# Softmax sums of an attention kernel: a chain of accumulating transfers, one meeting on TensorE, and the division on VectorE in PSUM

## The chip, the cores and the metric

The kernel runs on one core of a Trainium2 chip. The metric is device time in microseconds (us) of one execution; the time before is the median of three runs. A separate execution was recorded by the hardware profiler; all durations of single instructions come from that one. The engines are called PE (TensorE, matrix products), DVE (VectorE), ACT (ScalarE), POOL (GpSimd) and SP (the queue that issues most of the loads). Each engine works through its own instructions in the order in which the program wrote them, and waits on semaphores for the others.

## The reference

Two sequences of 2048 tokens with 512 features pass through a pre-norm attention layer and a small feed-forward layer.

```python
q = rope(layernorm(x) @ wq + bq)          # 16 heads of 32
k, v = rope(... @ wk + bk), ... @ wv + bv # 2 groups, each used by 8 heads
scores = einsum('bqhd,bkhd->bhqk', q * hd**-0.5, k) * hd**-0.5
attn = softmax(scores, axis=-1)
x = x + einsum('bhqk,bkhd->bqhd', attn, v) @ wo + bo
x = x + fp8_matmul(layernorm(x), weight)  # both operands rounded to e4m3
```

The softmax divides by the sum of the exponentials over all 2048 keys. The change is about how this sum is formed and how the division is done.

## The kernel before

**Tiling.** The tokens are cut into 8 blocks of 512 queries, and the 16 heads into 4 quads of 4 heads. A *unit* is one half block (256 queries) of one quad, so there are 64 units (`units`, L470). A unit runs over its 2048 keys in 4 *rounds* (`r` = 0 to 3, L994) of 4 chunks of 128 keys each. The main loop is L978 to L1034 and is unrolled; before it comes the projection of keys and of the first queries, and after it the last norms and the feed-forward layer.

**One chunk.** PE computes the scores of 4 heads into the PSUM tile `T` (L963), ACT writes `p = exp(T)` into SBUF, 128 keys x 4 heads x 256 queries (L972), and PE multiplies `p` by the values: `columns` (L905, L913) issues for each chunk 4 products, one for each head, that fill the 4 partition groups of `avs[:, 0, :]`. The four chunks' `columns` stand together at the end of the round (L1024).

**The maximum.** The exponentials need each row's maximum first. A generator, `scores_for_maxima` (L507), computes the scores once more for the *next* unit: PE writes `s` (L517), DVE reduces each to `part` (L524). The main loop advances it by four steps a round, two products and two reductions in each; the fourth step of a round (L1019) stands just before the filled-in jobs and `columns`. The steps run four ahead of the units, so a unit's last reduction, and `mx` (L531), fall in round 2 of the unit before it.

**The sums before.** POOL adds the exponentials of chunks 0 and 1 to `pair`, and of chunks 2 and 3 to a tile of `far_sums` (`add_pair`, L946). A transfer issued from POOL's queue then adds `pair` onto the far sum (L1015, `accum_op=add`), so that each round leaves one far sum. In round 2 one more such transfer adds `far_sums[0]` onto `far_sums[1]` (L1017). Three tiles remain. PE sums them over the 128 keys by products with a matrix of ones (`sum_up`, L923, L927): two of them at the end of the next unit's round 0, the third at the end of its round 1, into `avs[:, 1, :]`. Each tile takes 4 products, and a float32 product is two matmuls in the trace, so a unit has 24 of them.

**The division before.** `finish_heads` (L881) is a generator. When it is made, in round 1, ACT copies the sums from PSUM to SBUF (L885). Its further steps are run by `fill(ON_DVE, 3)` in the next round, round 2: two reciprocals of 128 columns each on DVE in SBUF (L889), and in the second of these steps the product on POOL (L890) that writes `attn_of`. At the end of each unit ACT copies `avs[:, 0, :]` to `both[:, 0, :]` (L1033).

**What sets the order.** The loop is written inside `manual_schedule`: each engine's order is the program's order. `fill` (L763) hands out other work between the fixed parts, one step at a time: first from `finishing`, then from `queue` (projections, output products `po`), then from `beside`. `fill(ON_DVE, ...)` at L1021 runs *after* the fourth scores step and *before* the round's `columns`. Waits between engines are not written by hand; the framework places them from what each instruction reads and writes.

**Buffers.** `avs` is a PSUM tile of 2 x 256 float32 per partition, 2048 bytes, with one buffer: its first half collects the products with the values of unit `u`, its second half the sums of unit `u - 1`. The tiles of `far_sums` have 4 buffers (tag `pa`), `p` has 4.

Of the kernel before, what the change touches and what calls it, by code (L numbers as in the profile page):

```python
# [8 lines left out]
F32 = mybir.dt.float32  # L9
# [4 lines left out]
ALU = mybir.AluOpType  # L14
AX = mybir.AxisListType

P = 128
# [10 lines left out]
def preln_attn_fp8_ffn_kernel(  # L28
# [37 lines left out]
    nc = tc.nc  # L66
# [9 lines left out]
    HB = 256  # L76
# [6 lines left out]
    ON_PE, ON_DVE, OTHER = "PE", "DVE", "other"  # L83
# [9 lines left out]
    w2 = ctx.enter_context(tc.tile_pool(name="w2", bufs=6))  # L93
# [376 lines left out]
    units = [(k, half) for k in range(len(quads)) for half in range(HALVES)]  # L470
# [133 lines left out]
    def finish_block(n, attn):  # L604
        yield OTHER
        xt = x_res.pop(n)
        for i in range(NT):
            yield from add_output(n, xt, attn, i)
        if n < len(y_far):
            nc.sync.dma_start(y_far[n], xt)  # L610
        else:
            y_near[n] = xt
        beside.append(Job(ending(second_norm(n, xt), f"res_{n}")))
        if n == NBLK - 2:
            fetch_y(0, xpool, "x")
            fetch_y(1, wide, "xnT")
            fetch_y(3, wide, "attn", bufs=2)


    def finish_most(n, xt, attn):  # L620
        yield OTHER
        for i in range(NT):
            yield from add_output(n, xt, attn, i, range(DC - 1))

    def finish_rest(n, xt, attn, half):
        yield OTHER
        tiles = range(half * HT, (half + 1) * HT)
        for i in tiles:
            yield from add_output(n, xt, attn, i, range(DC - 1, DC))
        beside.append(Job(second_norm(n, xt, tiles)))  # L630
        y_near[n] = xt
# [128 lines left out]
    finishing = []  # L760
    attn_of = {}

    def fill(kind, pieces=1):  # L763

        for _ in range(pieces):
            ready = [job for job in queue if job.due <= step[0] and not job.waits()]
            if lent[0] is not None:
                ready = [job for job in ready if job is owner[0]]
            able = [
                (jobs, job)  # L770
                for jobs, some in ((finishing, finishing[:1]), (queue, ready), (beside, beside))
                for job in some
                if job.kind in (kind, OTHER) and job.due <= step[0]
            ]
            if able:
                do(*able[0])

    def do(jobs, job):
        held = lent[0]
        job.step()  # L780
        if held is None and lent[0] is not None:
            owner[0] = job
        if job.kind is None:
            jobs.remove(job)
# [93 lines left out]
            fetch_y_over_keys(4, "kS", 0)  # L878
            fetch_y_over_keys(5, "dkS", 0)

    def finish_heads(u, both, sums):  # L881

        k, half = units[u]
        n, quad = quads[k]
        nc.scalar.copy(both[:, 1, :], sums)  # L885
        for c in range(HB // P):
            yield ON_DVE
            piece = both[:, 1, c * P : (c + 1) * P]
            nc.vector.reciprocal(piece, piece)  # L889
        nc.gpsimd.tensor_tensor(  # L890
            attn_of[n][:, quad, half * HB : (half + 1) * HB], both[:, 0, :], both[:, 1, :], ALU.mult
        )
        if n == NBLK - 1:
            if quad == QUADS - 2 and half == HALVES - 1:
                queue.append(Job(finish_most(n, x_res[n], attn_of[n])))
            elif quad == QUADS - 1:
                queue.append(Job(finish_rest(n, x_res[n], attn_of[n], half)))
        elif quad == QUADS - 1 and half == HALVES - 1:
            job = Job(finish_block(n, attn_of.pop(n)))
            if n not in biased:  # L900
                job.due = NEVER
                without_x[n] = job
            queue.append(job)

    def columns(u, chunks, probs, av):  # L905

        k, half = units[u]
        for kc, p in zip(chunks, probs):
            if kc == NTS - 2 and u + 1 < len(units):
                tp = ps_t.tile([P, 4 * HB], F32, tag="E", name=f"mtp_{u + 1}")  # L910
                gather_maxima(u + 1, tp)
            for j in range(4):
                nc.tensor.matmul(  # L913
                    av[j * HD : (j + 1) * HD, :],
                    vX[batch(k)][:, kc, group(k), :],
                    p[:, j, :],
                    start=(kc == 0),
                    stop=(kc == NTS - 1),
                    tile_position=(0, j * HD),
                    skip_group_check=True,  # L920
                )

    def sum_up(dst, parts, start, stop):  # L923

# [12 lines left out]
    def add_pair(u, kc, a, b):  # L937
        far = kc % ROUND == 2
        pa = papool.tile(
            [P, 4, HB],  # L940
            F32,
            tag="pa" if far else "pair",
            name=f"pa_{u}_{kc}",
            bufs=4 if far else 2,
        )
        nc.gpsimd.tensor_tensor(pa, a, b, ALU.add)  # L946
        return pa
# [27 lines left out]
    with tc.manual_schedule():  # L975
        for _ in range(LEAD):
            next(scores)
        for u, (k, half) in enumerate(units):  # L978
            n, quad = quads[k]
            if half == 0 and quad == 0:  # L980
                attn_of[n] = wide.tile(
                    [P, QUADS, TB], F32, tag="attn", name=f"attn_{n}", bufs=2
                )
            stack_next(u)
            banks = [
                ps_t.tile([P, 4, HB], F32, tag="EO"[parity], name=f"T_{u}_{parity}")
                for parity in range(2)
            ]

            far_sums = []  # L990
            whole = u == len(units) - 1
            ending_soon = u >= len(units) - 2
            pieces = 2 if ending_soon else 1
            for r in range(ROUNDS):  # L994
                chunks = list(range(r * ROUND, (r + 1) * ROUND))
                step[0] += 1
                while r == 1 and landing:
                    landing.pop()()
                if r == 2:
                    ask(u)  # L1000
                last = r == ROUNDS - 1
                next(scores, None)
                probs = [probabilities(u, banks[kc % 2], kc) for kc in chunks[:2]]
                pair = add_pair(u, chunks[0], *probs)
                next(scores, None)
                if r > 0:
                    fill(ON_PE, pieces)
                probs.append(probabilities(u, banks[0], chunks[2]))
                next(scores, None)
                probs.append(probabilities(u, banks[1], chunks[3]))  # L1010
                if ending_soon:
                    fill(ON_DVE)
                if not (last and whole):
                    far_sums.append(add_pair(u, chunks[2], *probs[2:]))
                    nc.gpsimd.dma_start(out=far_sums[r], in_=pair, accum_op=ALU.add)  # L1015
                if r == 2:
                    nc.gpsimd.dma_start(out=far_sums[1], in_=far_sums[0], accum_op=ALU.add)  # L1017
                fill(ON_PE, pieces)
                next(scores, None)  # L1019
                split_maxima()  # L1020
                fill(ON_DVE, 3 if finishing else 2)  # L1021
                if r == 0:
                    avs = ps_av.tile([P, 2, HB], F32, tag="av", name=f"avs_{u}")
                columns(u, chunks, probs, avs[:, 0, :])  # L1024


                if u > 0 and r == 0:
                    sum_up(avs[:, 1, :], far_before[1:3], False, False)
                elif u > 0 and r == 1:
                    sum_up(avs[:, 1, :], far_before[3:], False, True)  # L1030
                    finishing.append(Job(finish_heads(u - 1, both, avs[:, 1, :])))
            both = w2.tile([P, 2, HB], F32, tag="both", name=f"both_{u}", bufs=1)
            nc.scalar.copy(both[:, 0, :], avs[:, 0, :])  # L1033
            far_before = far_sums  # L1034
        sums = ps_s.tile([P, TB], F32, tag=s_bank(), name="sums_last")[:, :HB]
        sum_up(sums, [pair, *probs[2:], *far_sums[1:]], True, True)
        finishing.append(Job(finish_heads(u, both, sums)))
        fetch_y_over_keys(2, "kS", 1)
        attending[0] = False
        for jobs in (finishing, queue, beside):  # L1040
            while jobs:
                jobs[0].step()
                if jobs[0].kind is None:
                    jobs.pop(0)
# [122 lines left out]
```

## Time and profile before

| what | value |
|---|---|
| median of three runs | 2333.02 us (2332.41 to 2335.74) |
| the profiled execution | 2336.02 us, its span 2334.2 us |
| PE busy | 2143.7 us (92%) |
| DVE busy | 1698.0 us (73%) |
| ACT busy | 1237.0 us (53%) |
| POOL busy | 1765.1 us (76%) |
| mean granted TensorE clock | 0.970 |
| packets of the software queue (POOL's transfers) | 175.66 MB, 40.0% of the 16 engines' span |
| accumulating transfers `pa<-pa` | 319, 512.0 KB each, 4.9 us to landing (median) |

A group of the profile is given as line, engine, operation, output and inputs with their shapes and the count; then the busy time in total and the mean length of one in ns; then the idle time of the engine just before them and what ended it. The ends of matmuls are modelled, so a busy PE is not a PE at its peak. PEclk is the granted clock as a share of full speed. In the timeline, rows merge neighbouring instructions of one kind; the first column is the start in us, the second the length, and a bracket tells how long the engine had been idle and who released it.

### The profile page before, as it was taken

What the parts mean: (1) busy time and instruction counts of PE and PEld (TensorE: products, weight loads), DVE (VectorE), ACT (ScalarE), POOL (GpSimd) and SP (SyncE); (2) the same over time, 40 slices, a digit from 0 to 9 for tenths busy, and PEclk for the clock granted to TensorE, in tenths of its full rate; (3) what the DMA queues carried; (4) which work ended last, traced back from release to release, by engine and by line L of the source; (5) the groups of instructions that cost most, each with busy time, mean ns of one, the idle gap of its engine ahead of it and who ended that gap; (6) DMA issues with size and microseconds to landing.
All of it is one profiled execution on the core that took longest, in us unless ns stands there. A gap on an engine that the chain in (4) does not pass through costs nothing. (4 is left out here: it accounts for less than half of the span.)

```text
span 2334.2 us, 39403 instructions
## 1 busy us (share of the span) xinstructions
PE 2143.7 (92%) x15506; PEld 1242.2 (53%) x15506; DVE 1698.0 (73%) x2679; ACT 1237.0 (53%) x1545; POOL 1765.1 (76%) x1199
## 2 busy tenths in 40 slices
PE   5499999999999999999999999999999899899955
PEld 3255555555555555555555555555555455555522
DVE  3467778776777776876767778676877977767578
ACT  2146556655556555655445456555555555545646
POOL 3268889888878987888868878887888777877810
PEclk9599999999999999999999999999999999999978
DMA  6546656666465765659586456664665645847512
GB/s 204 160 102 128 141 114 161 140 142 131 100 163 130 159 129 136 145 115 197 103 202 137 102 127 136 147 112 96 133 154 123 138 101 115 170 98 197 109 52 112
DMA packets 116411, 312.78 MB, mean 134 GB/s; under 512 B 16896, under 2 KB 17536, under 8 KB 112384
## 3 DMA queue, kind: packets, MB, share of 16 engines
q0 software_dynamic: 50160, 175.66, 40.0%
q1 hardware_dynamic: 63648, 133.21, 19.2%
q8 instruction: 122, 2.00, 0.3%
q10 hardware_dynamic: 2416, 1.38, 0.2%
q14 instruction: 65, 0.53, 0.1%
HBM read 91.56 MB, written 42.99 MB: 58 GB/s over the span
## 5 line engine op out<-in xcount | busy, mean ns | idle before, releaser
L524 DVE TENSOR_REDUCE part<-s 128x1 f32<-128x512 f32 x2048 | 1304.2, 684 | 541.8 <-PE s L517 528.8
L946 POOL TENSOR_TENSOR pa<-p,p 128x1024 f32<-128x1024 f32 x511 | 1234.9, 2466 | 293.1 <-ACT p L972 265.8
L972 ACT ACTIVATE p<-T 128x1024 f32<-128x1024 f32 x1024 | 1001.4, 1024 | 597.8 <-PE T L963 564.6
L517 PE MATMUL s<-kS,qst 128*128 128x512 f32 x2048 | 832.1, 465 | 87.6 <-DVE part L524 28.7
L963 PE MATMUL T<-qst,dkS 128*128 128x512 f32 x2048 | 669.5, 423 | 11.8 <-ACT p L972 11.8
L517 PEld LDWEIGHTS s<-kS,qst 128*128 128x128 f32 x2048 | 369.7, 190 | 478.0 <-DVE part L524 266.5
L913 PE MATMUL avs<-p,vX 128*32 128x256 f32 x8192 | 509.4, 383 | 0.8 <-ACT p L972 0.8
L963 PEld LDWEIGHTS T<-qst,dkS 128*128 128x128 f32 x2048 | 366.0, 189 | 159.8 <-ACT p L972 54.8
L913 PEld LDWEIGHTS avs<-p,vX 128*32 128x32 f32 x8192 | 233.1, 109 | 214.4 <-issue 79.6
L1015 POOL DMA_DIRECT2D pa<-pa x255 | 224.2, 879 | 80.3 <-POOL pa L946 75.6
L301 PE MATMUL po<-wo_sb,attn 128*128 128x512 f32 x256 | 130.7, 596 | 1.3 <-POOL attn L890 1.3
L889 DVE RECIPROCAL both<-both 128x128 f32<-128x128 f32 x128 | 112.4, 920 | 11.2 <-ACT both L885 11.2
L301 PE MATMUL pq<-xnT_q,wq_sb 128*128 128x512 f32 x224 | 114.3, 592 | 0.0
L927 PE MATMUL avs<-pa,ones 128*32 128x256 f32 x1512 | 105.5, 382 | 5.5 <-DMA pa<-pa 5.5
L885 ACT COPY both<-avs 128x256 f32<-128x256 f32 x63 | 23.5, 372 | 132.8 <-PE avs L927 132.8
L890 POOL TENSOR_TENSOR attn<-both 128x256 f32<-128x256 f32 x64 | 85.2, 1331 | 5.9 <-DVE both L889 5.9
L954 PEld LDWEIGHTS T<-mT,sel 128*128 128x128 f32 x512 | 78.7, 190 | 13.6 <-ACT mT L546 1.9
L954 PE MATMUL T<-mT,sel 128*128 128x256 f32 x512 | 82.2, 283 | 1.1 <-ACT mT L546 1.1
L1017 POOL DMA_DIRECT2D pa<-pa x64 | 74.2, 1159 | 3.9 <-DMA pa<-pa 3.6
L927 PEld LDWEIGHTS avs<-pa,ones 128*32 128x32 f32 x1512 | 49.2, 111 | 38.6 <-DMA pa<-pa 6.0
L546 ACT CAST mT<-mtp 128x256 fp32r<-128x256 f32 x64 | 23.9, 373 | 84.0 <-PE mtp L542 84.0
L532 ACT CAST mrow<-mx 128x8 fp32r<-128x8 f32 x64 | 13.1, 205 | 93.5 <-DVE mx L531 93.5
(126 smaller groups left out, 1160.8 us busy)
## 6 DMA issues: line engine op xcount, KB each, us to landing
pa<-pa POOLq DMA_DIRECT2D x319, 512.0 KB, 4.9
qst<-q_far SPq DMA_DIRECT2D x128, 256.0 KB, 4.3
x_kv<-in_L_attn_x_dram SPq DMA_DIRECT2D x8, 1024.0 KB, 8.8
q_far<-hi_q SPq DMA_DIRECT2D x32, 256.0 KB, 4.4
q_far<-lo_q SPq DMA_DIRECT2D x32, 256.0 KB, 3.7
x_res<-in_L_attn_x_dram SPq DMA_DIRECT2D x8, 1024.0 KB, 8.2
x_res<-in_L_attn_bo_dram POOLq DMA_DIRECT2D x8, 1024.0 KB, 11.6
out_dram<-v SPq DMA_DIRECT2D x16, 512.0 KB, 2.8
```

The lines of the kernel that those rows point to most:

```text
L301: nc.tensor.matmul(dst, lhs(c), rhs(c), start=(c == 0), stop=(c == chunks - 1))
L517: nc.tensor.matmul(s, qst[k][:, j, at : at + P], stacked["kS"][:, group(k), kb * TB : (kb + 1) * TB], start=True, stop=True,)
L524: nc.vector.tensor_reduce(part[:, i, j, kb : kb + 1], s, AX.X, ALU.max)
L889: nc.vector.reciprocal(piece, piece)
L890: nc.gpsimd.tensor_tensor(attn_of[n][:, quad, half * HB : (half + 1) * HB], both[:, 0, :], both[:, 1, :], ALU.mult)
L913: nc.tensor.matmul(av[j * HD : (j + 1) * HD, :], vX[batch(k)][:, kc, group(k), :], p[:, j, :], start=(kc == 0), stop=(kc == NTS - 1), tile ...
L927: nc.tensor.matmul(dst[j * HD : (j + 1) * HD, :], ones, part[:, j, :], start=start and i == 0, stop=stop and i == len(parts) - 1, tile_pos ...
L946: nc.gpsimd.tensor_tensor(pa, a, b, ALU.add)
L954: nc.tensor.matmul(T[:, j, :], sel[:, j, :], maxima[u], start=(j % 2 == 0), stop=True, skip_group_check=True,)
L963: nc.tensor.matmul(T[:, j : j + 2, :], stacked["dkS"][:, group(k), kc * P : (kc + 1) * P], qst[k][:, j : j + 2, half * HB : (half + 1) * H ...
L972: nc.scalar.activation(p, T, AF.Exp, scale=SCALE)
L1015: nc.gpsimd.dma_start(out=far_sums[r], in_=pair, accum_op=ALU.add)
```

## The change

The unit's four far sums are now added up by transfers alone. In round 3 a transfer adds `far_sums[0]` onto `far_sums[1]`; in rounds 0 and 1 of the next unit two more add `[1]` onto `[2]` and `[2]` onto `[3]`. They are issued on POOL's queue just after the round's first pair addition. PE meets only `far_before[3]`, at the end of round 2 of the next unit. The old scheme stays for the last three units (`in_one`).

The division changes its place and its engine. ACT's copy of the sums is gone: the two reciprocals work in place on `avs[:, 1, :]` in PSUM, and a third step multiplies on DVE, from PSUM and SBUF, into `attn_of`; POOL's product is gone. As `sum_up` now stands at the end of round 2, these three steps are run by the `fill(ON_DVE, 4)` of round 3. `both` becomes `av`, with the first half alone.

```diff
-    def finish_heads(u, both, sums):
+    def finish_heads(u, av, sums):
...
-        nc.scalar.copy(both[:, 1, :], sums)
         for c in range(HB // P):
             yield ON_DVE
-            piece = both[:, 1, c * P : (c + 1) * P]
+            piece = sums[:, c * P : (c + 1) * P]
             nc.vector.reciprocal(piece, piece)
-        nc.gpsimd.tensor_tensor(
-            attn_of[n][:, quad, half * HB : (half + 1) * HB], both[:, 0, :], both[:, 1, :], ALU.mult
+        yield ON_DVE
+        nc.vector.tensor_tensor(
+            attn_of[n][:, quad, half * HB : (half + 1) * HB], av, sums, ALU.mult
         )
...
+    def in_one(u):
+
+        return 0 <= u < len(units) - 3
...
                 pair = add_pair(u, chunks[0], *probs)
+
+                if last and not whole or r < 2 and in_one(u - 1):
+                    far, at = (far_sums, 1) if last else (far_before, r + 2)
+                    nc.gpsimd.dma_start(out=far[at], in_=far[at - 1], accum_op=ALU.add)
...
-                if r == 2:
+                if r == 2 and whole:
                     nc.gpsimd.dma_start(out=far_sums[1], in_=far_sums[0], accum_op=ALU.add)
                 fill(ON_PE, pieces)
                 next(scores, None)
                 split_maxima()
-                fill(ON_DVE, 3 if finishing else 2)
+                fill(ON_DVE, 4 if finishing else 2)
                 if r == 0:
                     avs = ps_av.tile([P, 2, HB], F32, tag="av", name=f"avs_{u}")
                 columns(u, chunks, probs, avs[:, 0, :])
...
-                if u > 0 and r == 0:
+                if u > 0 and r == 0 and not in_one(u - 1):
                     sum_up(avs[:, 1, :], far_before[1:3], False, False)
-                elif u > 0 and r == 1:
+                elif u > 0 and r == (2 if in_one(u - 1) else 1):
                     sum_up(avs[:, 1, :], far_before[3:], False, True)
-                    finishing.append(Job(finish_heads(u - 1, both, avs[:, 1, :])))
-            both = w2.tile([P, 2, HB], F32, tag="both", name=f"both_{u}", bufs=1)
-            nc.scalar.copy(both[:, 0, :], avs[:, 0, :])
+                    finishing.append(Job(finish_heads(u - 1, av, avs[:, 1, :])))
+            av = w2.tile([P, HB], F32, tag="av", name=f"av_{u}", bufs=1)
+            nc.scalar.copy(av, avs[:, 0, :])
```

More of the change, by code (lines that the diff above doesn't have):

```diff
@@ L1036, in preln_attn_fp8_ffn_kernel @@
         sum_up(sums, [pair, *probs[2:], *far_sums[1:]], True, True)
-        finishing.append(Job(finish_heads(u, both, sums)))
+        finishing.append(Job(finish_heads(u, av, sums)))
         fetch_y_over_keys(2, "kS", 1)
```

## Prediction

> **What bounds the kernel now.** I read the page's busy row first, then the timeline of one unit in the middle, then the granted clock by stretches.
>
> ```profile
> PE 2143.7 (92%) x15506; PEld 1242.2 (53%) x15506; DVE 1698.0 (73%) x2679; ACT 1237.0 (53%) x1545; POOL 1765.1 (76%) x1199
> ...
> L889 DVE RECIPROCAL both<-both 128x128 f32<-128x128 f32 x128 | 112.4, 920 | 11.2 <-ACT both L885 11.2
> ...
> L927 PE MATMUL avs<-pa,ones 128*32 128x256 f32 x1512 | 105.5, 382 | 5.5 <-DMA pa<-pa 5.5
> ...
> L890 POOL TENSOR_TENSOR attn<-both 128x256 f32<-128x256 f32 x64 | 85.2, 1331 | 5.9 <-DVE both L889 5.9
> L1017 POOL DMA_DIRECT2D pa<-pa x64 | 74.2, 1159 | 3.9 <-DMA pa<-pa 3.6 <-issue 0.2
> ```
>
> PE sets the pace: nothing else is above 76%, and PE works in order, so what makes it wait is paid in full. From the first product of `columns` in one round to that in the next, I took from the timeline, as means over units 2 to 60: round 0 to 1 8.41 us, 1 to 2 7.97, 2 to 3 7.96, 3 to the next 0 8.62; some 33.0 us a unit.
>
> ```profile
> 1112.89 1.05 PE L927 MATMUL avs<-pa,ones 128*32 128x256 f32 x16
> 1113.87 0.73 PE L517 MATMUL s<-kS,qst 128*128 128x512 f32 x2
> ...
> 1129.08 1.75 DVE L889 RECIPROCAL both<-both 128x128 f32<-128x128 f32 x2
> ...
> 1135.06 1.03 PE L517 MATMUL s<-kS,qst 128*128 128x512 f32 x2
> 1135.89 1.29 DVE L524 TENSOR_REDUCE part<-s 128x1 f32<-128x512 f32 x2 [0.49 <-PE s L517]
> 1136.02 1.07 PE L913 MATMUL avs<-p,vX 128*32 128x256 f32 x16
> 1137.10 0.68 DVE L573 TENSOR_TENSOR x_res<-po,x_res 128x512 f32<-128x512 f32 x1
> ```
>
> The first two rows are the sums at the end of round 0: 16 matmuls hold PE for 0.98 us. The last four are the end of a round 3: `columns` starts at 1136.02, while DVE is still reducing (to 1137.18) and then does its jobs. PE owes nothing to those jobs today; DVE works beside `columns`.
>
> **Sums on PE.** 24 matmuls a unit become 8. Round 0 loses 0.98 us; of that I count 0.85, since DVE's jobs are sometimes the later ones there. Round 1 loses 8 matmuls, 0.54 us by the timeline (1121.37 to 1121.91); I count 0.5. Round 2 gains these 0.54 us. Together -0.81 us.
>
> **Reciprocals leave round 2.** Round 2 to 3 has no sums and yet takes as long as 1 to 2, which has 0.54 us of them: the 1.75 us of reciprocals delay the next scores by some 0.55 us there. Their move gives -0.55 us.
>
> **They arrive in round 3, on PE's path.** In program order they stand between the fourth scores step and `columns`. They now read and write `avs[:, 1, :]`; `columns` writes `avs[:, 0, :]`. Both halves are one 2048-byte piece of a partition. The Trainium skill, PSUM — Partial Sum Buffer, "PSUM bank collisions raise a hardware error", says that a bank is 2 KiB, that TensorE and VectorE must not be in one bank and quadrant together even at disjoint columns, and that one guards by bank and quadrant, not by address. So I take it that `columns` of round 3 waits until DVE has done both reciprocals and the product. The trace before cannot show it: there ACT copied the sums out at once (L885, 0.37 us), a round before the next `columns`. By the rows alone, with DVE beside `columns` as now, the sum would be a gain; by the rule it is this stall: DVE ends its last reduction 1.0 us after the present start of `columns` (mean over the units; 1.16 above); two reciprocals 1.75 us in SBUF, in PSUM between 1.75 and 1.9 (a reduction reads PSUM at 684 ns, L524, and SBUF at 671, L587), taken 1.8; the product of 256 columns between 0.33 and 0.67 (half and whole of the 668 ns of L573 for 512), by the slope to 1226 ns for 1024 columns (L239) 0.39, taken 0.4; release of PE by DVE 0.05. Sum +3.25 us. Queued behind the stalled `columns` on PE are the transposes of the maxima and all of the next unit's products, hence everybody. What DVE does after it (0.99 us of other jobs a round 3) now hides behind `columns`: -0.25, by the share of about a third with which such jobs lengthen a round now.
>
> **The clock.** The stall leaves PE idle for some 3.2 us.
>
> ```profile
> 1189.77 0.72 PE L517 MATMUL s<-kS,qst 128*128 128x512 f32 x2
> ...
> 1193.31 0.62 PE L517 MATMUL s<-kS,qst 128*128 128x512 f32 x2
> ...
> 1200.43 1.19 PE L517 MATMUL s<-kS,qst 128*128 128x512 f32 x2 [2.85 <-DMA qst<-q_far]
> ...
> 1206.54 0.67 PE L517 MATMUL s<-kS,qst 128*128 128x512 f32 x2
> ```
>
> ```profile
> 1196.40:1199.80 3.40, 1.17 (x24) 0.43 (x16) 2.26 (x4) 0.21 (x1) 3.10 (x3) 1.00 0.99 268
> 1199.80:1203.20 3.40, 2.77 (x7) 2.25 (x8) 1.29 (x2) 0.63 (x1) 1.20 (x3) 0.50 1.00 213
> 1203.20:1206.60 3.40, 3.40 (x8) 2.00 (x7) 1.29 (x2) 1.31 (x2) 3.13 (x4) 0.50 0.92 176
> 1206.60:1210.00 3.40, 3.40 (x26) 1.79 (x25) 2.48 (x4) 1.96 (x2) 1.46 (x2) 1.00 0.02 4
> ```
>
> The columns of the second view are length, busy time of PE, PEld, DVE, ACT and POOL, then PEclk. A single gap of 2.85 us, 2.23 of it in one stretch of 3.4 us, halved the clock for two stretches. The same products took 6.11 us (1200.43 to 1206.54) instead of 3.54: 0.42 us lost for each us worked at half clock. Looking through all such stretches, those with 1.96 us or more idle were all followed by half clock, one with 1.53 and one with 1.83 were not. The skill, TensorE: Matmul & The Clock Gate, "HAM oscillation", asks for no gap over about 3.4 us, and says that the window runs freely; by its figure a 3.2 us gap would mostly pass and nothing be added. The row decides: a 3.2 us gap falling anywhere on such stretches leaves 1.85 us in one of them five times in six. With the second stretch at half clock wherever 0.6 us of the gap spill into it (as at 1199.8), I get 3.4 us worked at half clock per unit on average, times 0.42 = +1.45 us.
>
> **POOL, ACT, transfers.** POOL loses a 1331 ns product and gets 122 more issues in all, two a unit. An issue's row is 0.87 to 1.18 us, but the next instruction starts 0.6 us after it, so POOL comes out even: -1.33 + 1.2. The issues go ahead of the far addition, which ACT's `p` of the next round needs; POOL's 24% of idle time covers 0.6 us, and without cover a unit would pay up to 1.8. Each chain transfer waits on POOL for the one a round earlier: 8 us against a landing of 4.9 us (median); only near large loads (up to 16.3 us) does it bind, some 4 us in all. The 122 x 512 KB more, 62 MB, raise the software queue's share by 14 points (62/175.66 of its 40.0%); `qst` is fetched over a unit ahead and hides it. ACT's copy (0.37 us) was off the path: nothing.
>
> **Sum.** -0.81 - 0.55 + 3.25 - 0.25 + 1.45 = +3.1 us a unit; 61 units give 189. The last units, with the old sums but the new division, add about 5, the transfers 4, the end saves 1.5 (ACT's copy and POOL's product). 2334.2 + 196 = 2530 us of span; the profiled execution was 1.8 us over its span and 3 over the median, so the median comes out at 2530 as well.
>
> **Rivals.** (1) The stall with the halved clock, as summed: 2530, chance 0.60, own range 2465 to 2600. (2) The stall, but the clock holds, because PE's gaps stay under what trips it: 2530 - 88 = about 2440, chance 0.25. For it: the 1.83 us stretch that passed, and a stall some 0.6 us shorter would split oftener. (3) Other side: PE does not wait, or for less than 1.6 us, since the framework orders by address and DVE works beside `columns`: then -0.81 - 0.55 a unit, 61 x -1.4 = -86, 2250. It decides from a stall under 1.6 us; the reciprocals alone take 1.75. Against it stands the rule; chance 0.05. (4) The stall and more: the removed sums were only cover for DVE (nothing gained, +82), or the chain lands late and POOL holds `p` up (1.4 us a unit, +85): about 2615, chance 0.10. For it: L1017 waits and PE's 5.5 us on `pa<-pa`; against it the 8 us of room.
>
> **Range.** 2425 to 2600: it leaves out (3), half of (4) and the edges of (1) and (2). Within 0.2% is about what this measurement can tell from no change: faster 0.05, same 0.01, slower 0.94.
>
> **What would show it.** After: PE or PEld `avs L913` waits for DVE in round 3, some 3 us at 63 places; PEclk clearly below 0.97, near 0.9, with drops once a unit; L927 in `avs` at 536 matmuls (61 x 8 + 2 x 24); DVE's `attn` product near 0.4 us. Wrong I am if `columns` of round 3 starts before DVE's product ends, or if PE waits and the clock stays at 0.97.

## The result, and the profile after

The changed kernel takes 2636.26 us (median of four runs, 2626.07 to 2639.09) against 2332.72 us: 1.129 times the time before, with a 95% interval of 1.126 to 1.133. The profiled execution has a span of 2634.3 us and a mean granted clock of 0.916, where 2334.2 us and 0.970 stood before. It was forecast to become slower, but by 197 us, not by 303; the measured time lies 36 us above the range.

Rows of the page of the changed kernel, in the columns explained above: the busy row, `columns` (L913), the chain's transfers (L1011), the reciprocals (L888) and the sums (L931):

```profile
PE 2217.8 (84%) x14530; PEld 1258.6 (48%) x14530; DVE 1758.2 (67%) x2743; ACT 1211.9 (46%) x1481; POOL 1825.0 (69%) x1257
...
L913 PE MATMUL avs<-p,vX 128*32 128x256 f32 x8192 | 596.3, 431 | 228.2 <-DVE attn L890 218.9
...
L1011 POOL DMA_DIRECT2D pa<-pa x185 | 165.5, 895 | 34.5 <-DMA pa<-pa 34.3
...
L888 DVE RECIPROCAL avs<-avs 128x128 f32<-128x128 f32 x126 | 121.1, 961 | 7.1 <-PE avs L931 4.9
...
L931 PE MATMUL avs<-pa,ones 128*32 128x256 f32 x536 | 42.7, 394 | 11.7 <-DMA pa<-pa 11.6
```

The sums did shrink, from 1512 matmuls to 536. But every engine's share fell, PE's from 92% to 84%, and PE now sits idle for 218.9 us in front of `columns` until DVE's product L890 is done; before, that line had 0.8 us of idle time in all:

```profile
L913 PE MATMUL avs<-p,vX 128*32 128x256 f32 x8192 | 509.4, 383 | 0.8 <-ACT p L972 0.8
```

The timeline of one round 3 in the changed kernel:

```profile
1312.09 1.02 PE L517 MATMUL s<-kS,qst 128*128 128x512 f32 x2
...
1312.92 1.29 DVE L524 TENSOR_REDUCE part<-s 128x1 f32<-128x512 f32 x2 [0.50 <-PE s L517]
...
1314.13 1.96 DVE L888 RECIPROCAL avs<-avs 128x128 f32<-128x128 f32 x2
1316.12 0.42 DVE L890 TENSOR_TENSOR attn<-av,avs 128x256 f32<-128x256 f32 x1
...
1316.60 1.94 PE L913 MATMUL avs<-p,vX 128*32 128x256 f32 x16 [3.48 <-DVE attn L890]
```

DVE reduces, divides and multiplies, and only then does PE begin `columns`, 3.48 us after it had fallen idle. The first 16 matmuls of `columns` then take 1.94 us where they took 1.07 before. The reason is in the view by stretches (length, busy time of PE, PEld, DVE, ACT and POOL, PEclk, share and rate of the transfers) around the same stall:

```profile
1309.50:1313.00 3.50, 3.50 (x13) 1.96 (x11) 2.25 (x5) 2.84 (x3) 2.53 (x2) 1.00 0.61 115
1313.00:1316.50 3.50, 0.11 (x1) 0.00 (x0) 3.43 (x5) 0.00 (x0) 3.20 (x3) 0.89 0.70 135
1316.50:1320.00 3.50, 3.40 (x30) 1.35 (x34) 0.04 (x1) 0.37 (x1) 0.67 (x1) 0.50 0.79 150
1320.00:1323.50 3.50, 3.50 (x23) 2.42 (x16) 1.29 (x2) 1.06 (x3) 1.14 (x1) 0.64 0.23 64
```

PE is idle in the second stretch, and the clock is at one half in the third and part of the fourth. From unit 2 to the start of unit 60, which is 58 units, there were 63 drops to half clock, 310.6 us in all; before there were 4, 23.9 us. Of the 58 stalls, 55 were followed by a drop; the other 8 drops lie elsewhere, four of them in a round in which PE also waited for the chain.

Round by round, from the first product of one `columns` to that of the next (means over the same units, us):

| from round | before | after | forecast of the difference | difference |
|---|---|---|---|---|
| 0 to 1 | 8.43 | 7.70 | -0.85 | -0.73 |
| 1 to 2 | 7.99 | 7.66 | -0.50 | -0.33 |
| 2 to 3 (holds the stall) | 7.99 | 12.07 | +3.24 | +4.08 |
| 3 to 0 (holds the half clock) | 8.64 | 10.38 | +1.20 | +1.74 |
| a unit | 33.05 | 37.81 | +3.09 | +4.76 |

4.76 us for 61 units is 290 of the 303 us.

### The profile page after: what moved, and what is told of

Same layout as the page of the kernel before. It is cut to its first block, busy times and chain, and to the rows that moved or that the text cites. A ratio compares the mean times of both kernels' runs of the same rounds, so it can differ in the third digit from the quotient of the medians.

```text
span 2634.3 us, 37607 instructions
## 1 busy us (share of the span) xinstructions
PE 2217.8 (84%) x14530; PEld 1258.6 (48%) x14530; DVE 1758.2 (67%) x2743; ACT 1211.9 (46%) x1481; POOL 1825.0 (69%) x1257
## 4 chain that ended last, share of the span: by engine, by line
PE 56%; DVE 20%; DMA 8%; POOL 6%; ACT 5%; issue 3%; SPq 1%; DVEq 0%; ACTq 0%; POOLq 0%
PE avs L913 16%; PE s L517 15%; PE T L967 12%; DVE part L524 10%; DMA pa<-pa 6%; DVE avs L888 4%; ACT p L976 4%; POOL pa L950 4%; PE po L301 3%; PE pq L301 3%; PE T L958 2%; DVE sw_q L319 2%; PE mtp L542 1%; PE avs L931 1%; DVE attn L890 1%
## 5 line engine op out<-in xcount | busy, mean ns | idle before, releaser
L950 POOL TENSOR_TENSOR pa<-p,p 128x1024 f32<-128x1024 f32 x511 | 1283.0, 2525 | 401.8 <-ACT p L976 384.9
L913 PE MATMUL avs<-p,vX 128*32 128x256 f32 x8192 | 596.3, 431 | 228.2 <-DVE attn L890 218.9
L913 PEld LDWEIGHTS avs<-p,vX 128*32 128x32 f32 x8192 | 249.5, 119 | 486.2 <-DVE attn L890 243.1
L1022 POOL DMA_DIRECT2D pa<-pa x255 | 223.6, 877 | 82.8 <-POOL pa L950 68.9
L1011 POOL DMA_DIRECT2D pa<-pa x185 | 165.5, 895 | 34.5 <-DMA pa<-pa 34.3
L888 DVE RECIPROCAL avs<-avs 128x128 f32<-128x128 f32 x126 | 121.1, 961 | 7.1 <-PE avs L931 4.9
L247 POOL TENSOR_TENSOR lo_q<-q,hi_q 128x512 fp32r<-128x512 f32 x32 | 41.0, 1280 | 93.9 <-ACT hi_q L246 93.7
L319 DVE SCALAR_TENSOR_TENSOR sw_q<-sw_q,sign,cs 128x512 f32<-128x512 f32 x30 | 68.8, 2294 | 0.7 <-issue 0.5
L1040 ACT COPY av<-avs 128x256 f32<-128x256 f32 x64 | 23.9, 374 | 89.4 <-PE avs L913 89.4
L301 PEld LDWEIGHTS po<-wo_sb,attn 128*128 128x128 f32 x256 | 49.1, 192 | 13.0 <-issue 3.9
L931 PE MATMUL avs<-pa,ones 128*32 128x256 f32 x536 | 42.7, 394 | 11.7 <-DMA pa<-pa 11.6
```

Of the source, the lines that this page charges most:

```text
L301: nc.tensor.matmul(dst, lhs(c), rhs(c), start=(c == 0), stop=(c == chunks - 1))
L319: nc.vector.scalar_tensor_tensor(t[:rows], t[:rows], sign[:rows], csb[:rows, 1, :], ALU.mult, ALU.mult)
L913: nc.tensor.matmul(av[j * HD : (j + 1) * HD, :], vX[batch(k)][:, kc, group(k), :], p[:, j, :], start=(kc == 0), stop=(kc == NTS - 1), tile ...
L1011: nc.gpsimd.dma_start(out=far[at], in_=far[at - 1], accum_op=ALU.add)
```

## Experiments

The theory: (a) PE waits because the division stands in front of `columns` in the same PSUM bank (the framework places that wait; here the bank and the tile `avs` are the same 2048 bytes, and no run tells a wait by bank from a wait by tile); (b) the idle PE loses its clock; and, since (a) and (b) as forecast leave 106 us over, one of them is larger than forecast or (c) the longer chain of transfers costs something. The rivals make the chain, or DVE's extra work as such, the main cause. All results are medians beside runs of the kernel before on the same chip (2331.64 to 2334.13 us).

### e1: the division in SBUF

```diff
+        nc.scalar.copy(both[:, 1, :], sums)
...
-            piece = sums[:, c * P : (c + 1) * P]
+            piece = both[:, 1, c * P : (c + 1) * P]
...
-            attn_of[n][...], av, sums, ALU.mult
+            attn_of[n][...], both[:, 0, :], both[:, 1, :], ALU.mult
```

> The changed kernel, but ACT copies the sums out of PSUM as in the kernel before, and the reciprocals and the product work in SBUF, still on DVE and in round 3. Theory (columns waits for DVE because both are in one PSUM bank, and the clock falls in that gap): no wait of avs L913 on DVE, PEclk back at 0.97, 2270 to 2320 us. Rival (the longer chain of transfers and its issues on POOL cost the time): still over 2450 us. Rival (DVE's extra work as such): still over 2550 us.

Measured: 2393.26 us, ratio to the kernel before 1.026 (1.024 to 1.028), clock 0.959. The waits of `columns` for DVE are gone, and 243 us with them: (a) holds for the greater part. But 60 us of loss remain where a gain of 10 to 60 was expected: there is something else in the change that costs.

### e2: the division alone

```diff
 (kernel before)
-        nc.scalar.copy(both[:, 1, :], sums)
...
-            piece = both[:, 1, c * P : (c + 1) * P]
+            piece = sums[:, c * P : (c + 1) * P]
...
-        nc.gpsimd.tensor_tensor(
-            attn_of[n][...], both[:, 0, :], both[:, 1, :], ALU.mult
+        yield ON_DVE
+        nc.vector.tensor_tensor(
+            attn_of[n][...], av, sums, ALU.mult
...
-                fill(ON_DVE, 3 if finishing else 2)
+                fill(ON_DVE, 4 if finishing else 2)
```

> The kernel before with the division alone changed: reciprocals and product on DVE, in PSUM, run in round 2; the sums as before (three tiles on PE, one extra transfer). Theory (the wait in the bank): PE waits some 3.5 us in every unit's round 2, the clock falls each time, nothing is gained on the sums: 2620 to 2700 us. Rival (the chain of transfers): 2330 to 2360 us.

Measured: 2621.43 us, 1.124 (1.122 to 1.126), clock 0.926; PE waits 3.67 us on average in front of the `columns` of round 2 (who waited for whom: us in total, times, longest):

```profile
PE avs L913 <- DVE attn L890: 227.6, 62, 3.9
```

With the sums untouched, the division alone brings 289 us: nearly the whole loss, and only 15 us less than the full change. The new way of summing, for all the PE time that it saves, seems to bring nothing on top. The two differ in one thing more, since the division falls in round 2 here and in round 3 there. By the medians of the rounds the changed kernel takes 0.87 us a unit less than e2, by their means 0.19 more, which points to single late rounds that use up what the sums save.

### e3: PE kept at work in the stall

Twelve products whose results nobody uses stand in front of the `columns` of round 3.

```diff
+                if last and 0 < u < len(units) - 2:
+                    for _ in range(12):
+                        nc.tensor.matmul(banks[0][:, 0:2, :], stacked["kS"][:, group(k), :P],
+                            qst[k][:, 0:2, half * HB : (half + 1) * HB], start=True, stop=True, ...)
                 columns(u, chunks, probs, avs[:, 0, :])
```

> The changed kernel with twelve products more (128x512, some 2.8 us, results unused, into a PSUM tile that is finished with) in front of the columns of round 3 of units 1 to 61, where PE would sit idle for 3.5 us. If the halved clock costs what the timeline after suggests (4.3 us a unit at half clock, times 0.42): PEclk near 0.97 and 2500 to 2540 us. If it costs what was forecast (1.45 us a unit): about 2550. If the clock costs nothing: 2636, no change.

Measured: 2532.30 us, 1.086 (1.083 to 1.089). PE does 732 products more and is 104 us faster than the changed kernel.

```profile
L913 PE MATMUL avs<-p,vX 128*32 128x256 f32 x8192 | 515.7, 385 | 56.3 <-DVE attn L890 47.4 <-ACT p L976 8.9
...
L1033 PE MATMUL T<-qst,kS 128*128 128x512 f32 x732 | 177.9, 392 | 3.9 <-ACT p L976 3.7
```

These groups of e3 show that `columns` takes 385 ns a matmul again, not 431, while the stall itself stays: rounds 2 to 3 take 12.21 us (12.07 in the changed kernel), rounds 3 to 0 8.45 instead of 10.38. The clock is at 0.969. So the halved clock cost 1.93 us in this row of each unit (1.75 over the whole unit, 37.81 to 36.06): (b) holds, and is larger than the 1.45 forecast.

### e8: the division behind `columns`

The same three instructions on the same PSUM tile, but behind the unit's last `columns` and ACT's copy, with two buffers of `av`.

```diff
-                    finishing.append(Job(finish_heads(u - 1, av, avs[:, 1, :])))
+                    done = finish_heads(u - 1, av, avs[:, 1, :])
...
             nc.scalar.copy(av, avs[:, 0, :])
+            if u > 0:
+                for _ in done:
+                    pass
```

> The changed kernel, the division still on DVE and in PSUM, but its three instructions stand behind the last columns of the unit and behind ACT's copy (two buffers of av), not in front of them. Theory (PE loses time only because columns stands behind the division in the same bank): no wait of avs L913 on DVE, PEclk near 0.96, 2370 to 2420 us like e6 (2381), the rest of the loss being the late chain. Rival (division in PSUM on DVE is dear wherever it stands): over 2550 us.

Measured: 2393.18 us, 1.027 (1.024 to 1.029), clock 0.964. The row of `columns` in e8:

```profile
L913 PE MATMUL avs<-p,vX 128*32 128x256 f32 x8192 | 510.4, 383 | 1.1 <-ACT p L976 1.1
```

It no longer waits for DVE at all. With the division still on DVE and still in PSUM, moving three instructions within the program is worth 243 us: it was their place in front of `columns` that was dear. They are not free behind it either. From round 3 to 0 e8 takes 10.18 us, against 8.64 in the kernel before:

```profile
1238.40 1.97 DVE L888 RECIPROCAL avs<-avs 128x128 f32<-128x128 f32 x2 [0.34 <-ACT av L1040]
...
1240.40 0.42 DVE L890 TENSOR_TENSOR attn<-av,avs 128x256 f32<-128x256 f32 x1
1240.74 4.96 DVE L524 TENSOR_REDUCE part<-s 128x1 f32<-128x512 f32 x8
1241.48 0.50 PE L517 MATMUL s<-kS,qst 128*128 128x512 f32 x1 [0.77 <-DVE part L524]
```

DVE divides before it takes up the next unit's reductions, and PE's scores wait for these. So the 60 us that e8 still loses are not the late chain alone, as the expectation had it.

### e4: the division a round later, alone

```diff
 (kernel before)
+                elif u > 0 and r == 2:
                     finishing.append(Job(finish_heads(u - 1, both, avs[:, 1, :])))
-            both = w2.tile(..., bufs=1)
+            both = w2.tile(..., bufs=2)
```

> The kernel before with the division a round later alone (copy of the sums at the end of round 2, reciprocals in SBUF and POOL's product in round 3; two buffers of both, so that ACT's copy at the unit's end waits for nobody). If reciprocals in round 2 cost 0.55 us that round 3 hides, as forecast: 2295 to 2315 us. If other DVE jobs take their place in round 2 or round 3 does not hide them: 2325 to 2345 us.

Measured: 2316.12 us, 0.993 (0.991 to 0.995): faster than both kernels. Rounds 2 to 3 fall from 7.99 to 7.49 us, rounds 3 to 0 rise from 8.64 to 8.81. The relief forecast as 0.55 us is there in the first of these rows; 0.17 of it comes back in the second.

### e5, e6, e7 and e11: the chain

e6 is e1 with two buffers of `both`. e7 is e6 with the product on POOL, as before; it differs from e4 only in the sums, by two transfers a unit more and 16 matmuls fewer, and in the place of the old link, which e12 below finds to cost nothing. e5 is e6 without the chain's last link, PE summing two tiles at the end of round 2. e11 is e7 without that link, PE summing the two at the end of round 1.

```diff
 (e5, against e6)
-                if last and not whole or r < 2 and in_one(u - 1):
+                if last and not whole or r < 1 and in_one(u - 1):
...
-                    sum_up(avs[:, 1, :], far_before[3:], False, True)
+                    sum_up(avs[:, 1, :], far_before[2 if in_one(u - 1) else 3 :], False, True)
```

> As e1 with two buffers of both, so that ACT's copy at the end of a unit no longer waits for DVE's product (118 us of ACT waiting in e1). If that wait cost e1 its gain: 2290 to 2330 us. If the late chain did: 2370 to 2390 us, PE still waiting for pa transfers about nine times.

> As e6, but POOL makes the product as in the kernel before (so only the chain of transfers and the round differ from before). If the product's place matters little: within 15 us of e6. If DVE is the one that is short: 20 to 40 us below e6. If POOL, which issues the chain, is short: 20 us or more above e6, with more waits of PE for pa transfers.

> As e6 (division in SBUF on DVE in round 3, two buffers of both), but the chain without its last link: no transfer in round 1, PE sums two tiles (16 matmuls) at the end of round 2. Theory (in e1 the chain landed too late: PE waited for it 9 times for 3.5 us, and the clock fell after each): those waits vanish, half clock back to about 25 us in units 2 to 60, and though PE has 0.5 us a unit more to do, 2285 to 2320 us, below e6. Rival (the landings cost nothing, e1's loss is ACT's or DVE's): e6 plus some 30 us.

> As e7 (2369 us) without the link of round 1: PE sums the two tiles left (16 matmuls) at the end of round 1, division in round 3, product on POOL. One transfer a unit more than in e4, 8 matmuls fewer. Theory (e7 loses to links that wait on POOL for a landing, and to PE waiting for the last of them): about 2310 to 2335 us, POOL's waits for pa transfers down to less than half of e7's. Rival (it is the traffic as such): about 2340 to 2360.

Measured: e6 2381.30 us, 1.021 (1.020 to 1.023). ACT's waiting in e1 was worth only 12 us. e7 2368.66 us, 1.016 (1.014 to 1.019): 13 us below e6, within the 15 us of "matters little", and 52 us *slower* than e4, though PE has less to do. By the medians of its rounds e7 takes 0.8 us a unit less than e4, as much as the sums were forecast to save, by their means 0.80 us more: it loses in single rounds. The waits of e4, and then of e7 (who waited for whom: us in total, times, longest):

```profile
ACT p L972 <- POOL pa L946: 55.1, 22, 4.2
...
PE avs L927 <- DMA pa<-pa: 6.7, 1, 6.7
```

```profile
ACT p L976 <- POOL pa L950: 97.1, 45, 8.0
...
PE avs L931 <- DMA pa<-pa: 32.4, 10, 5.3
POOL pa L1011 <- DMA pa<-pa: 27.9, 14, 4.8
```

One of these places in e7's timeline:

```profile
1255.70 0.87 POOL L1011 DMA_DIRECT2D pa<-pa  x1 [4.06 <-DMA pa<-pa]
...
1256.30 2.67 POOL L950 TENSOR_TENSOR pa<-p,p 128x1024 f32<-128x1024 f32 x1
...
1259.00 1.94 ACT L976 ACTIVATE p<-T 128x1024 f32<-128x1024 f32 x2 [2.06 <-POOL pa L950]
```

A link waits on POOL's queue 4.06 us for the landing of the one before it; the addition behind it is late, so ACT's exponentials are. Where PE itself waits, it waits about 3 us, and the clock drops: 81.9 us at half clock in units 2 to 60, against 23.9 in e4. The landing takes 5.0 us in the median in e7 as in e4, but 54 of 441 take over 8 us, up to 14.2; in e4 it is 35 of 319. Of the 54, 34 ran beside a transfer of a megabyte, as only 93 of the 441 did. The share of late landings hardly grows (11 to 12%); there are more of them, and more waits behind each. A chain with one link a round leaves room for the median, not for these.

e5, 2366.66 us, 1.014 (1.012 to 1.016), does not decide: the waits of PE for transfers vanish as expected, but POOL's addition of round 2 reuses the buffer that PE now reads at that round's end, and waits for it (103.6 us, 47 times). e11 avoids that: 2339.72 us, 1.003 (1.002 to 1.004), 29 us below e7. POOL's waits on the links fall from 27.9 to 1.9 us, but other additions on POOL wait for landings longer (56.5 us instead of 38.0), and PE still 24.8 us. It ends between the two expectations, and whether the waits or the traffic as such make its remaining 24 us over e4 stays open.

### e10 and e12: what is left of the change

> As e4 (old sums, division in SBUF in round 3; 2316 us) with the product on DVE in place of POOL. If POOL's time matters: 2300 to 2312 us. If DVE's does: 2318 to 2330. If neither: within 4 us of 2316.

e10 is e4 with POOL's product moved to DVE (`nc.vector.tensor_tensor` after one `yield ON_DVE` more, and four steps for `fill`). Measured: 2336.74 us, 1.002 (1.001 to 1.003), 21 us above e4 and 7 above the range expected if DVE's time mattered. The product's row in e10, and one of the long products in its timeline:

```profile
L891 DVE TENSOR_TENSOR attn<-both 128x256 f32<-128x256 f32 x64 | 58.3, 911 | 2.2
...
769.44 4.74 POOL L947 TENSOR_TENSOR pa<-p,p 128x1024 f32<-128x1024 f32 x2
...
772.25 2.21 DVE L891 TENSOR_TENSOR attn<-both 128x256 f32<-128x256 f32 x1
```

From two SBUF tiles it takes 911 ns in the mean, against 421 with one input in PSUM in the changed kernel. Single ones run from 424 (the median is 426) to 3268 ns in e10, and from 420 to 423 in the changed kernel. All 25 products of e10 that take over 0.5 us began while POOL was at work and ended 0.28 to 0.30 us after an instruction of POOL's had ended (above, 774.46 after 774.18): they are held up until it is done.

> As e4 (2316 us) with the one extra transfer moved from round 2 to round 3, behind the pair addition, as the change does; no transfer more, no matmul fewer. If the place of a link on POOL's queue is what makes it dear: 2325 to 2345 us, with more waits of PE or POOL for pa transfers. If only additional links cost: 2310 to 2322 us.

e12 is e4 with the one old link moved from round 2 to round 3, at the place of the change. Measured: 2315.42 us, 0.993 (0.991 to 0.995), like e4. A link's place is not what costs; by e7 against e4, links on top are.

## Why the prediction was right and wrong

**The stall** (+3.25 us, of +3.24 in the row of round 2 to 3) was right in its place, its cause and nearly in its size: 3.52 us of idle PE on average. The bank rule read from the skill decided here over the rows, and e8 and e1 show that the wait comes and goes with the division's place in `avs` ahead of `columns`. That the guard goes by bank rather than by tile is not shown; the two are the same here. The two reciprocals take 1.96 us in PSUM, above the upper bound of 1.9 that was given; the product took 0.42 us, where 0.4 was taken.

**The reciprocals leaving round 2** (-0.55): right; e4 shows -0.50 in that row. **The sums**: right in kind, 0.29 us a unit too large for rounds 0 and 1 (-1.06 measured, -1.35 forecast), in the changed kernel.

**The clock** (+1.45) was right that it drops, and mis-sized: e3 measures 1.93 us a unit in that row, 104 us in the run. The step that failed is the time at half clock. I reckoned 3.4 us worked at half clock a unit; it was 4.26 us in each round 3 to 0. The price of 0.42 us for each us so worked held nearly (1.93 for 4.26 is 0.45), and so did the marks read from the stretches.

Laid over the stretches of 3.41 us on which the granted clock changes, the 58 stalls divide by their split: the three that passed had at most 1.93 us idle in either stretch, and of the 55 that brought a drop all but one (1.80) had 1.95 us or more in one. The 24 drops of two stretches followed stalls that had 2.01 us or more in the first stretch and ran on for 0.48 to 1.61 us into the next. By the forecast's own marks (1.85 us and 0.6 us, a gap of 3.2 us falling anywhere) these would have been about one stall in five, 0.75 of 3.41; with gaps of 3.5 us, at the places where they fell, they were 24 of 58.

At 3.47 to 3.63 us these gaps also lie just above the skill's figure of about 3.4, so it is the gap of 2.85 us before that speaks against that figure, and not they. (That the window runs freely stands on the skill's page under "What's actually happening"; the split of the gap did decide here.)

**The transfers** (4 us in all) is the other step that failed. The chain was judged by the median landing of 4.9 us against a room of 8 us. e7 against e4 puts the new sums at +52 us, where the sums' own terms, -1.35 + 0.54 a unit, promise -49: some 100 us for late landings and what follows them. In the changed kernel itself the units are longer and give more room: 2621 for the division alone (e2, in round 2) against 2636 with the new sums leaves +15 us where -49 were promised. At five places its round 2 to 3 is late by 25 us in all beyond the median one, each with `avs L931` waiting for the chain and four with half clock in the same round. Rival (4) named the late chain, on POOL, at a chance of 0.10; it came on top of rival (1), rather than in its place, and a range made from one case at a time did not reach it.

Of the 106 us that the forecast fell short, the table gives 102, or 1.67 us a unit: 0.84 in round 2 to 3 (0.27 a longer stall, 0.43 those late places, the rest unassigned), 0.54 in round 3 to 0 (0.48 the clock) and 0.29 in the other two (the sums).

**Rival (3)**, that PE would not wait, fell; e8 is what it would have taken. The marks given beforehand all appeared: 62 waits (63 forecast) of `columns` for DVE, 536 sums, a clock of 0.916. In sum the loss is mainly one wait: 243 us go with it (e8, e1), and 104 us go when the clock alone is kept (e3). The 60 us left in e1 are ACT's wait for its buffer (12, e6), the product on DVE (13, e7), and 36 that e7 still loses to the kernel before: there the chain is dearer than all that PE saves by it.

## What to carry to other kernels

Before an operation is left in PSUM to save a copy, look for what the writer of the *same bank* (here also the same tile) has queued behind it in program order: a copy of 0.37 us that empties the bank at once was worth far more here than it cost, and the order alone was worth as much. Price an idle gap of the matrix engine together with the clock that follows it. And judge a chain of dependent transfers by its late landings, not by the median, when something in order waits behind each link.

## What the runs showed of the hardware

Twelve unused products in each of 61 stalls made the changed kernel 104 us faster, by keeping the clock. The clock halves on gaps below the 3.4 us that the Trainium skill (TensorE: Matmul & The Clock Gate, "HAM oscillation") asks one to avoid: in the kernel before a gap of 2.85 us did it, and 1.96 us idle in one stretch of 3.4 us always sufficed; of the changed kernel's stalls all with 1.95 us or more in one stretch were followed by half clock, and three of the four with 1.80 to 1.93 were not; in e2 all 15 stalls of 3.33 to 3.40 us were followed by it. A product of 128x256 on DVE took 420 to 423 ns with one input in PSUM, and 424 to 3268 ns (e10; up to 3317 in e1) with both in SBUF. The skill's page SBUF — State Buffer, "Who interferes with whom", says that DVE with two SBUF inputs and POOL reading SBUF take one port pair in turns, each for a whole instruction. The traces agree: POOL's additions take 2.3 to 3.8 us in the kernel before, all 25 long products of e10 ended just behind an instruction of POOL's, and in the changed kernel, with one input in PSUM, 27 of the 64 products began while POOL was at work and none was held up.
